# A graph network with attention on one core: where GpSimd adds the output bias and forms block sums

## The chip, the core and the metric

The kernel runs on one core of one Trainium2 chip. The time is the device time of one execution in microseconds (us); lower is better. TensorE (PE) multiplies into PSUM banks, ScalarE (ACT) and VectorE (DVE) read them out, GpSimd (POOL) works on SBUF alone here, and SyncE (SP) issues nearly all DMAs. Each engine works through its own queue in order and waits on semaphores.

## The reference

Everything is float32. `N` is 1024 nodes, `D` 512, there are `L` = 4 layers, 8 heads and 16 graphs of 64 nodes with 256 condition rows each.

```python
h = relu(layernorm(x)); x_in = h
h = batchnorm(h) * bn_w + bn_b
h = gcn(h, src, dst, gcn_in_w, gcn_in_b)
for i in range(4):
    a = attn(ln(h, ln2_w[i], ln2_b[i]), cond, Wq[i], Wk[i], Wv[i], Wo[i])
    h = h + a
    u = ln(h, ln3_w[i], ln3_b[i]) @ geglu_w[i] + geglu_b[i]      # 512 -> 4096
    val, gate = split(u, 2)
    f = val * gelu(gate)                                         # exact gelu
    h = h + f @ ffo_w[i] + ffo_b[i]                              # 2048 -> 512
h = gcn(h, src, dst, gcn_out_w, gcn_out_b)
return x + h + x_in
```

The bias `ffo_b[i]` is a term of a sum: it may be added to `h` anywhere behind the layer's second normalisation (`ln3`) and ahead of the next layer's first (`ln2`).

## The kernel before, in words

**Products.** Nearly every product is written as seven block products in place of eight (a fast scheme over 2 x 2 blocks). Each operand needs three or four extra sums or differences of its blocks ahead of the product, and VectorE adds the results up as they leave PSUM. The operand sums are what GpSimd mostly does:

- `weight_sums` (L220 to L223, tiles `wks`, `wvs`, `wqs`) for the attention's weights,
- `wo_sums` (L838, into the tile `wos`) for the output projection,
- `sum_first` (`sums_of_b`, L213 to L216, tiles `ln2T`, `ln2S`) for the normalised rows; blocks 0 and 1 on GpSimd, 2 and 3 on VectorE,
- `pair_sums` (L848 to L851) and parts of `attn_out_pair` for the attention's output,
- `ln3_sums` (tiles `ln3T`, `ln3S`) behind the second normalisation,
- `geglu_weights` (L220 to L223, tiles `ges`), `inner_left` (tiles `gi`), `inner_right` (L987, into `wos` once the attention no longer needs it) and `out_weights` (tiles `wffs`) for the feed-forward part.

**A layer.** `h` lies in SBUF as eight row blocks of 128 (`h[0]` to `h[7]`, views of the tile `hall`).

1. *Start of a layer.* For every layer but the first: `weight_sums` for the queries, `sum_first` of blocks 0 and 1 on GpSimd, then `kv(l, 0, ...)`: the keys of the first group, on VectorE behind their last copy `ready_first(l, left_to_turn[2:])` (mean, variance, reciprocal root in some ten steps on 128x2 numbers at L134 to L143, and the scaled rows at L172), and the values. Then `turn_first` transposes the four blocks left over, VectorE makes the sums of blocks 2 and 3 (L213 to L216), and `queries` follows. `wo_sums` is issued behind the last of the GpSimd sums (`summed`).
2. *Attention.* A loop over `g` = 0 to 7, a group being two graphs. Behind the keys of group `g + 1` the function `between` adds the attention's output of two earlier blocks to `h` and normalises the blocks in `ready` (`ln3_norm`): block `g - 2`, and blocks 4 and 5 when `g` is 6. Blocks 6 and 7 are normalised behind the loop.
3. *Feed-forward part*, in four quarters `r` = 0 to 3 of the 2048 inner columns. In each, `geglu` makes the gated product and `ffn_out` multiplies it by the quarter's `ffo_w` and adds into `h` in two halves `s` (blocks 0, 1, 4, 5 and blocks 2, 3, 6, 7; L1116). In the quarter `r` = 0 the gated product is made by four quads (`Quad.rest`, L938 to L957; the last operation, L957, is returned by the lambda). Behind each quad VectorE makes a block sum of the result (L1085, or L1087 to L1089). In the quarters `r` >= 1 it is made by two pairs (`Pair.run`), in which two of the seven block products (`INNER`, 5 and 6) are again split into seven (`Pair.seven`); these need `inner_left` sums of the weights, new in each quarter, and `inner_right` sums of the normalised rows, which are made once, behind the first quarter, and kept in `wos`. L1063, L964 and L968 are VectorE's additions in a pair.

Behind the first quarter's `geglu.last` (L1089) GpSimd makes `geglu_weights` for `r` = 1, then `inner_blocks` (left and right), `out_weights` for `r` = 1, and in `r` = 1 the eight bias adds at L1405. They are written ahead of the second quarter's pairs:

```python
            if r == 1:
                for nb in range(NB):
                    nc.gpsimd.tensor_tensor(h[nb], h[nb], ffb, OP.add)
```

**Order.** The order of each queue comes from the order of the program text, priorities, and two helpers. `tc.issue_after(ins)` puts what is inside behind an instruction in the queues. `waiting_for(ins, engine)` makes every instruction of that engine inside it wait for `ins` by a semaphore. SBUF tiles come from pools of fixed size, so a load waits until the tile that lay there before is done with; the biases `ffb` and `bias_out` share the pool `rows` with two places, and the next layer's `ffb` is loaded when the one before it has been used.

Of the kernel before, what the change touches and what calls it, by code (L numbers as in the profile page):

```python
# [14 lines left out]
OP = mybir.AluOpType  # L15
# [8 lines left out]
def gnn_kernel(  # L24
# [26 lines left out]
    nc = tc.nc  # L51
# [3 lines left out]
    BS, M, DC = cond.shape  # L55
# [162 lines left out]
    def sums_of_a(t, a11, a12, a21, a22, s1, s2, s4):  # L218

        t.tensor_tensor(s1, a21, a22, OP.add)  # L220
        t.tensor_tensor(a21, a11, a21, OP.subtract)
        t.tensor_tensor(s2, s1, a11, OP.subtract)
        t.tensor_tensor(s4, a12, s2, OP.subtract)  # L223

    def halves_of(t):
        return t.rearrange("p (a b) -> p a b", a=2)
# [474 lines left out]
    def weight_sums(w, name):  # L701

        s = slots_of(2, name)
        blk = blocks_of_w(w)
        s1, s2, s4 = (halves_of(s[i // 2][:, i % 2, :]) for i in range(3))
        sums_of_a(nc.gpsimd, *blk, s1, s2, s4)
        return [blk[0], blk[1], s4, blk[3], s1, s2, blk[2]]

    def seven(name, product, c11, c12, c21, c22, s1=None, beside=lambda ins: None,
# [273 lines left out]
    def inner_right(t, y, t1, t2, t3, t4):  # L983

        b11, b12, b21, b22 = (y[:, k, n * M:(n + 1) * M] for k in range(2) for n in range(2))
        for to, of, less in ((t1, b12, b11), (t3, b22, b12), (t2, b22, t1), (t4, b21, t2)):
            t.tensor_tensor(to, of, less, OP.subtract)  # L987
        return [b11, b21, b22, t4, t1, t2, t3]

    INNER = (5, 6)  # L990

    def inner_blocks(l, r, left, right, rights):

        rooms = [t512(f"gi_{l}_{r}_{i}") for i in range(3)]
        rooms = [x[:, i * M:(i + 1) * M] for x in rooms for i in range(2)]
        kept = [wos[:, n, i * M:(i + 1) * M] for n in range(4) for i in range(2)]
        lefts = {}
        for n, i in enumerate(INNER):
            if not r:
                rights[i] = inner_right(nc.gpsimd, right[i], *kept[4 * n:4 * n + 4])  # L1000
            lefts[i] = inner_left(nc.gpsimd, left[i], *rooms[3 * n:3 * n + 3])
        return lefts

    class Pair:

# [73 lines left out]
    def geglu(quads, fT, s, begun, beside=lambda c: None):  # L1079
        def sums(c):  # L1080
            k = c % 2
            a11, a12, a21, a22 = (fT[i][j][:, k, :] for i in range(2) for j in range(2))
            s1, s2, s4 = (x[:, k, :] for x in s)
            if c < 2:
                nc.vector.tensor_tensor(a21, a11, a21, OP.subtract)  # L1085
            else:
                nc.vector.tensor_tensor(s2, a22, a21, OP.subtract)  # L1087
                nc.vector.tensor_tensor(s1, s2, a11, OP.add)
                sums.last = nc.vector.tensor_tensor(s4, a12, s2, OP.subtract)  # L1089

        for c, q in enumerate(quads):
            if begun:
                q.rest()()
                beside(c)
                sums(c)
            else:
                q.run(sums, beside)
        geglu.last = sums.last
        return order7([*fT[0], *fT[1]], *s)
# [165 lines left out]
    for l in range(L):  # L1265

        wk, wv, wq, wo, ffb = projections
        if l:
            wq = weight_sums(wq, f"wqs_{l}")
            lnS = slots_of(3, f"ln2S_{l}")  # L1270
            sum_first(nc.gpsimd, 0)
            summed = sum_first(nc.gpsimd, 1)
            kv_next = kv(l, 0, wk, wv, lambda _: ready_first(l, left_to_turn[2:]))
            turn_first(l, left_to_turn)
            next_cond(l, 1)
            sum_first(nc.vector, 2)
            sum_first(nc.vector, 3)
        else:
            lnS = slots_of(3, f"ln2S_{l}")
            roots = []  # L1280

            def root_beside(ins):
                with tc.issue_after(ins.ins):
                    roots.append(deviations(mv_first[1], "ln2_0_4"))

            kT, last_key = keys(0, 0, wk, begun["k0"], root_beside)
            with tc.issue_after(last_key.ins):
                scale_first(1, *roots)
            turn_first(0, [0, 1, 2, 3])
            with waiting_for(scale_first.last, mybir.EngineType.Pool):  # L1290
                wq = weight_sums(wq, "wqs_0")
            kv_next = kT, values(0, 0, wv, begun["v0"])
            turn_first(0, [4, 5, 6, 7])
            sum_first(nc.gpsimd, 0)
            summed = sum_first(nc.gpsimd, 1)
            kT_1, last_key = keys(0, 1, wk, begun["k1"])
            with tc.issue_after(last_key.ins):
                sum_first(nc.vector, 2)
                sum_first(nc.vector, 3)
# [19 lines left out]
        def ln3_sums(t, nb):  # L1319
# [2 lines left out]
            of = [ln3T[i][k][:, :, c0:c0 + P] for k in range(2) for i in range(2)]  # L1322
            sums_of_b(t, *of, *(x[:, :, c0:c0 + P] for x in ln3S), nc.gpsimd)

        oTs = []
        for g in range(NG - 1):
            kT, v = kv_next
            if g == NG - 2:
                raw = load_geglu(l, 0)
            if l == 0:  # L1330
                fetch_cond(g + 2)
            probs = scores(l, g, qT, kT)
            ready = [g - 2, g - 1] if g == NG - 2 else [g - 2] if g > 1 else []

            def between(last_key):
                nonlocal left
                if len(oTs) == 2:
                    blocks = pair_sums(l, g - 2, oTs)
                    oTs.clear()
                    if g == NG - 2:  # L1340
                        with waiting_for(scores.last, mybir.EngineType.Pool):
                            left = geglu_weights(l, 0, *raw)
                    attn_out_pair(l, g - 2, *blocks, wo7)
                ln3_norm(*ready, behind=last_key)

            if g or l:
                kv_next = kv(l, g + 1, wk, wv, between, late=lambda: [ln3_turn(nb) for nb in ready])
            else:
                kv_next = kT_1, values(0, 1, wv)
            save_conds()  # L1350
            next_cond(l, g + 2)
            for nb in ready:
                if nb >= 4:
                    ln3_sums(nc.gpsimd, nb)
            oTs.append(mix(l, g, probs, v))
# [42 lines left out]
        for r in range(R):  # L1398
            if r:
                wff = out_weights(nc.gpsimd, l, r, raw_out)  # L1400
            else:
                raw_out = load_out(l, 0)
            if r == 1:
                for nb in range(NB):
                    nc.gpsimd.tensor_tensor(h[nb], h[nb], ffb, OP.add)  # L1405
            if r + 1 < R:
                raw = load_geglu(l, r + 1)
            beside = lambda c: None
            if r:
                fT, fS, quads = pairs_of(l, r, left, right, (lefts, rights))  # L1410
                nb = 2 * (l * (R - 1) + r - 1)
                if nb < NB:
                    if nb == 0:
                        bias_out = load_row(gcn_out_b, 0, "bias_out")
                        nc.gpsimd.tensor_tensor(x_shift, x_mean.rearrange(
                            "p a (b c) -> p (a b) c", c=2)[:, :, 0], x_root, OP.mult)
                        nc.gpsimd.tensor_scalar(x_shift, x_shift, -1.0, None, OP.mult)
                    fetch_x(nb)
                    fetch_x(nb + 1)
                    beside = lambda p: base_of(nb + p)  # L1420
            else:
                wff = []
                beside = lambda c: wff.extend(
                    out_weights(nc.vector, l, 0, raw_out) if c == 2 else [])
            fT = geglu(quads, fT, fS, not r, beside)
            if r + 1 < R:
                raw_out = load_out(l, r + 1)
                with waiting_for(geglu.last, mybir.EngineType.Pool):
                    left = geglu_weights(l, r + 1, *raw)
                    lefts = inner_blocks(l, r, left, right, rights)  # L1430
                for s in range(2):
                    ffn_out(l, r, s, fT, wff, kept)
            else:
                lnT = [slots_of(2, f"ln2T_{l + 1}_{i}") for i in range(2)]
                if last:
                    w_out, base = load_last()
                else:
                    projections = load_projections(l + 1)
                ffn_out(l, r, 0, fT, wff, kept)
                ready_first(l + 1, [0, 1, 4, 5])  # L1440
                ffn_out(l, r, 1, fT, wff, kept)
                turn_first(l + 1, [0, 1, 4, 5])
                left_to_turn = [2, 3, 6, 7]
                ready_first(l + 1, left_to_turn[:2])
# [58 lines left out]
```

## Time and profile before

| | us |
|---|---|
| median of three runs | 2542.27 |
| lowest and highest of them | 2540.95, 2543.8 |
| the profiled execution, its own time | 2546.36 |
| its span in the trace | 2544.6 |
| busy in the span: TensorE | 2498.3 |
| VectorE | 1519.7 |
| GpSimd | 614.7 |
| ScalarE | 533.4 |

The mean granted TensorE clock over the span is 0.996. In the rows of the profile, "L1405" is a line of the kernel, "x7" a number of instructions that a row merges, and `hall<-hall,ffb` the tile written and the tiles read. In a timeline the first two numbers are the start from the span's begin and the time taken, and what stands in brackets is the idle time ahead of the row on its engine and who ended it. In the waits the numbers are the sum, how often, and the longest. In the groups the first two numbers behind the bar are the busy time and the mean of one in ns, and behind the second bar stands the idle time ahead of the group.

### The profile page before, as it was taken

Reading aid. Unit: us, or ns where it says so; the run is one execution under the profiler, and the core shown is the slowest. Engines: PE = TensorE matmul, PEld = TensorE weight load, DVE = VectorE, ACT = ScalarE, POOL = GpSimd, SP = SyncE. Lnnn points to the kernel's source line nnn. Section 1 sums busy time; section 2 is a strip of 40 time slices with the busy share of each in tenths; the row PEclk is TensorE's granted clock in tenths of the full one; section 3 lists DMA queues with packets and bytes.
Section 4 is the critical chain, followed back from the end, with each engine's and each line's share of the span. In section 5 each row is a group of like instructions: output and inputs, shape, how many; then the busy total and the mean of one; then the engine's idle time right before and its main releaser. Section 6 shows DMA issues by size and latency. Waiting matters only on the chain. (4 is left out here: it accounts for less than half of the span.)

```text
span 2544.6 us, 33047 instructions
## 1 busy us (share of the span) xinstructions
PE 2498.3 (98%) x12752; PEld 1824.1 (72%) x12752; DVE 1519.7 (60%) x3298; ACT 533.4 (21%) x1318; POOL 614.7 (24%) x581
## 2 busy tenths in 40 slices
PE   7999999999999999999999999999999999999999
PEld 5778886666668887666677888566677888566665
DVE  9655565656764555666584555655584555665561
ACT  7322222111112222111112222210112222211111
POOL 1322222544310003352420003053420002153300
PEclk9999999999999999999999999999999999999999
DMA  6302231111211122110202211110121122111210
GB/s 178 130 29 92 92 128 51 42 67 33 103 52 65 59 63 67 42 67 17 96 29 75 71 63 56 44 42 26 50 75 58 47 70 67 42 42 50 83 34 34
DMA packets 69380, 161.06 MB, mean 63 GB/s; under 512 B 5768, under 2 KB 6096, under 8 KB 69216
## 3 DMA queue, kind: packets, MB, share of 16 engines
q1 hardware_dynamic: 67120, 153.44, 18.5%
q0 software_dynamic: 1376, 4.30, 0.5%
q8 instruction: 105, 1.72, 0.3%
q10 hardware_dynamic: 720, 1.11, 0.1%
q14 instruction: 59, 0.48, 0.1%
HBM read 135.76 MB, written 23.07 MB: 62 GB/s over the span
## 5 line engine op out<-in xcount | busy, mean ns | idle before, releaser
L302 PE MATMUL ga<-ln3T,wval 128*128 128x512 f32 x512 | 246.5, 595 | 0.0
L302 PEld LDWEIGHTS ga<-ln3T,wval 128*128 128x128 f32 x512 | 96.4, 191 | 90.4 <-issue 86.5
L933 ACT ACTIVATE g<-g,gcols 128x512 f32<-128x512 f32 x128 | 87.2, 716 | 341.4 <-DVE g L964 113.8
L777 ACT ACTIVATE pr<-sc,nmax 128x256 f32<-128x256 f32 x256 | 118.0, 473 | 176.7 <-DVE nmax L772 176.7
L848 POOL TENSOR_TENSOR os<-oT 128x256 f32<-128x256 f32 x12 | 8.7, 728 | 586.3 <-DVE oT L823 586.3
L220 POOL TENSOR_TENSOR ges<-wgate,wgate 128x1024 f32<-128x1024 f32 x16 | 37.7, 2356 | 412.6 <-DVE fs L1089 312.4
L302 PE MATMUL pd_k<-ct,wks 128*128 128x256 f32 x512 | 125.1, 389 | 8.8 <-DVE y_ln L136 8.8
L302 PE MATMUL gd<-ln3T,ges 128*128 128x512 f32 x256 | 123.5, 605 | 9.7 <-DVE g L964 9.6
L302 PE MATMUL gd<-ln3S,ges 128*128 128x512 f32 x256 | 128.1, 592 | 0.0
L302 PE MATMUL pa_v<-wv,ct 128*128 128x256 f32 x512 | 124.1, 382 | 0.0
L302 PE MATMUL fa<-wff,fT 128*128 128x256 f32 x512 | 121.6, 379 | 0.0
L302 PE MATMUL pc_v<-wv,ct 128*128 128x256 f32 x512 | 121.0, 379 | 0.0
L302 PE MATMUL pc_k<-ct,wk 128*128 128x256 f32 x512 | 121.0, 379 | 0.0
L302 PE MATMUL pd_v<-wvs,ct 128*128 128x256 f32 x512 | 120.9, 379 | 0.0
L302 PE MATMUL gc<-ln3S,wgate 128*128 128x512 f32 x256 | 120.3, 592 | 0.0
L302 PEld LDWEIGHTS pd_k<-ct,wks 128*128 128x128 f32 x512 | 99.4, 195 | 23.9 <-issue 9.9
L302 PE MATMUL pa_k<-ct,wk 128*128 128x256 f32 x480 | 116.2, 385 | 0.0
L302 PEld LDWEIGHTS fa<-wff,fT 128*128 128x128 f32 x512 | 97.3, 190 | 21.8 <-issue 8.9
L302 PEld LDWEIGHTS pa_v<-wv,ct 128*128 128x128 f32 x512 | 98.1, 192 | 14.0 <-issue 0.4
L302 PEld LDWEIGHTS pc_k<-ct,wk 128*128 128x128 f32 x512 | 97.3, 190 | 13.2
L302 PEld LDWEIGHTS pd_v<-wvs,ct 128*128 128x128 f32 x512 | 97.3, 190 | 13.2
L302 PEld LDWEIGHTS pc_v<-wv,ct 128*128 128x128 f32 x512 | 95.7, 190 | 12.2
(354 smaller groups left out, 5079.4 us busy)
## 6 DMA issues: line engine op xcount, KB each, us to landing
ct<-cond_dram SPq DMA_DIRECT2D x72, 512.0 KB, 4.4
wval<-in_L_gnn_geglu_w_dram SPq DMA_DIRECT2D x32, 512.0 KB, 3.8
wgate<-in_L_gnn_geglu_w_dram SPq DMA_DIRECT2D x32, 512.0 KB, 4.7
wff<-in_L_gnn_ffo_w_dram SPq DMA_DIRECT2D x32, 512.0 KB, 4.1
cond_dram<-ct SPq DMA_DIRECT2D x24, 512.0 KB, 3.2
cond<-in_L_gnn_cond_dram SPq DMA_DIRECT2D x32, 256.0 KB, 4.5
ct<-cond_dram SPq DMA_DIRECT2D x24, 256.0 KB, 5.4
wk<-in_L_gnn_Wk_dram SPq DMA_DIRECT2D x8, 512.0 KB, 4.6
```

The costliest lines, as they stand in the source:

```text
L220: t.tensor_tensor(s1, a21, a22, OP.add)
L302: nc.tensor.matmul(at, left[:, k, l0:l1], right[:, k, r0:r1], start=start and n == 0 and k == 0, stop=n == len(cols_of) - 1 and k == 1, sk ...
L777: nc.scalar.activation(pr3[:, a, :], ps3[:, a, :], AF.Exp, bias=nmax[:, a:a + 1], accum_out=tot[:, a:a + 1])
L848: t.tensor_tensor(s1, a21, a22, OP.add)
L933: nc.scalar.activation(pre, pre, AF.Gelu, bias=gcols[:, cg:cg + 1])
```

## The change

1. **Output bias.** The eight adds of `ffb` to `h` in the quarter `r` = 1 are gone. `add_bias` adds it to a block on GpSimd right behind that block's second normalisation in the attention (blocks 0 to 5), and for blocks 6 and 7 behind the first quarter's gated product, together with the sums for `r` = 1. In the built queue of GpSimd these two stand second and fifth there, between the four `ges` sums.
2. **Right sums.** `inner_blocks` is divided. The left sums stay where they were. The right sums are made during the first quarter: those of product 5 wait for quad 0's last operation, those of product 6 for quad 1's.
3. **First sums of a layer** (layers 1 to 3). `sum_first` of blocks 0 and 1 and the queries' `weight_sums` are written behind `kv(l, 0, ...)` and wait for `scaled.last`, the last scaled rows of the layer's first normalisation. `wo_sums` now comes behind the last of the queries' weight sums.

TensorE, ScalarE and VectorE keep their instructions and, but for one exchange of two neighbouring products in the first quarter's output and of the two additions that belong to them, their order. In SyncE's queue the load of the next layer's `ffb` moves, in layers 0 and 1, from behind the weights for `r` = 2 to ahead of the two loads `x_again` that stand before those weights.

```diff
@@ sums_of_a
-        t.tensor_tensor(s4, a12, s2, OP.subtract)
+        return t.tensor_tensor(s4, a12, s2, OP.subtract)
@@ weight_sums
-        sums_of_a(nc.gpsimd, *blk, s1, s2, s4)
+        weight_sums.last = sums_of_a(nc.gpsimd, *blk, s1, s2, s4)
@@
-    def inner_blocks(l, r, left, right, rights):
-
+    def inner_lefts(l, r, left):
         rooms = [t512(f"gi_{l}_{r}_{i}") for i in range(3)]
         rooms = [x[:, i * M:(i + 1) * M] for x in rooms for i in range(2)]
-        kept = [wos[:, n, i * M:(i + 1) * M] for n in range(4) for i in range(2)]
-        lefts = {}
-        for n, i in enumerate(INNER):
-            if not r:
-                rights[i] = inner_right(nc.gpsimd, right[i], *kept[4 * n:4 * n + 4])
-            lefts[i] = inner_left(nc.gpsimd, left[i], *rooms[3 * n:3 * n + 3])
-        return lefts
+        return {i: inner_left(nc.gpsimd, left[i], *rooms[3 * n:3 * n + 3])
+                for n, i in enumerate(INNER)}
+
+    def inner_right_of(n, right):
+        rooms = [wos[:, 2 * n + k, i * M:(i + 1) * M] for k in range(2) for i in range(2)]
+        return inner_right(nc.gpsimd, right[INNER[n]], *rooms)
@@ geglu
-                q.rest()()
+                q.last = q.rest()()
@@ start of a layer
         if l:
-            wq = weight_sums(wq, f"wqs_{l}")
             lnS = slots_of(3, f"ln2S_{l}")
-            sum_first(nc.gpsimd, 0)
-            summed = sum_first(nc.gpsimd, 1)
             kv_next = kv(l, 0, wk, wv, lambda _: ready_first(l, left_to_turn[2:]))
+            with waiting_for(scaled.last, mybir.EngineType.Pool):
+                sum_first(nc.gpsimd, 0)
+                sum_first(nc.gpsimd, 1)
+                wq = weight_sums(wq, f"wqs_{l}")
+                summed = weight_sums.last
             turn_first(l, left_to_turn)
@@ attention
+        def add_bias(nb):
+            nc.gpsimd.tensor_tensor(h[nb], h[nb], ffb, OP.add)
+
@@ between
                 ln3_norm(*ready, behind=last_key)
+                for nb in ready:
+                    add_bias(nb)
@@ quarters
-            if r == 1:
-                for nb in range(NB):
-                    nc.gpsimd.tensor_tensor(h[nb], h[nb], ffb, OP.add)
@@
                 wff = []
-                beside = lambda c: wff.extend(
-                    out_weights(nc.vector, l, 0, raw_out) if c == 2 else [])
+
+                def beside(c):
+                    if c == 2:
+                        wff.extend(out_weights(nc.vector, l, 0, raw_out))
+                    elif c < 2:
+                        with waiting_for(quads[c].last, mybir.EngineType.Pool):
+                            rights[INNER[c]] = inner_right_of(c, right)
+
             fT = geglu(quads, fT, fS, not r, beside)
             if r + 1 < R:
                 raw_out = load_out(l, r + 1)
                 with waiting_for(geglu.last, mybir.EngineType.Pool):
                     left = geglu_weights(l, r + 1, *raw)
-                    lefts = inner_blocks(l, r, left, right, rights)
+                    lefts = inner_lefts(l, r + 1, left)
+                    if not r:
+                        for nb in range(NB - 2, NB):
+                            add_bias(nb)
```

## The prediction

> **What bounds the kernel now.** I read the page first, then the waits of TensorE, then the granted clock around each wait, then the timeline in front of each.
>
> ```profile
> PE 2498.3 (98%) x12752; PEld 1824.1 (72%) x12752; DVE 1519.7 (60%) x3298; ACT 533.4 (21%) x1318; POOL 614.7 (24%) x581
> ```
>
> TensorE is busy for 98% and the queues of its work stay as they are, so a change elsewhere can only move the 2% in which it waits, and what follows a wait. Who it waits for:
>
> ```profile
> PE gd L302 <- DVE g L964: 9.6, 4, 2.4
> PE pd_k L302 <- DVE y_ln L136: 8.8, 3, 3.0
> PE tr_ln L184 <- DVE xn_ln L172: 5.4, 4, 1.7
> ```
>
> The first is one wait per layer, the second one per layer but the first. Both are VectorE being late. A wait also costs after its end, which the windows show (the column behind the busy times is PEclk, the granted clock):
>
> ```profile
> 508.00:513.00 5.00, 4.73 (x7) 2.01 (x8) 3.13 (x6) 2.65 (x4) 1.89 (x2) 0.66 0.03 11
> 709.00:714.00 5.00, 4.49 (x25) 4.07 (x26) 4.79 (x14) 2.94 (x7) 2.85 (x5) 1.00 0.08 30
> 1100.00:1105.00 5.00, 4.42 (x11) 2.03 (x12) 4.03 (x5) 2.65 (x4) 1.57 (x2) 1.00 0.08 22
> 1905.00:1910.00 5.00, 4.34 (x13) 3.63 (x14) 4.33 (x15) 0.00 (x0) 0.00 (x0) 0.66 0.01 3
> ```
>
> A mean of 0.66 over 5 us is 3.4 us at half clock: 5 x 0.34 = 1.7 us of TensorE's work lost. It came behind two of the four L964 waits (508 is the first; behind 1100 there is none) and all three L136 waits (1905 is the last), five in all: 8.5 us. Behind the shorter tr_ln wait (709) the clock stayed at 1.00. The Trainium skill (TensorE: Matmul & The Clock Gate, "Part 1: The HAM clock gate") says that the gate halves the clock after about one idle window of 3.4 us; by that no wait of 2.4 to 3.0 us would lower it and the 8.5 us would be left out of the sum. The trace differs: 2.4 us were enough twice, so the rows decide.
>
> **Why VectorE is late in the second quarter (r = 1).**
>
> ```profile
> 497.20 8.61 POOL L1405 TENSOR_TENSOR hall<-hall,ffb 128x512 f32<-128x512 f32 x7
> ...
> 502.51 3.85 DVE L1063 TENSOR_TENSOR gw<-gw,gw 128x512 f32<-128x512 f32 x1
> ...
> 508.27 2.83 PE L302 MATMUL gd<-ln3T,ges 128*128 128x512 f32 x4 [2.39 <-DVE g L964]
> ...
> 530.08 0.69 DVE L1063 TENSOR_TENSOR gw<-gw,gw 128x512 f32<-128x512 f32 x1
> ```
>
> L1063 adds two SBUF tiles. It takes 0.69 us when GpSimd is idle (530.08) and 3.85 us while seven bias adds run: it ends 0.55 us after their end at 505.81. TensorE's wait of 2.39 us is shorter than the 3.16 us that L1063 loses, so without the adds L964 is 0.8 us early.
>
> **Why it is late at a layer's start.**
>
> ```profile
> 715.41 0.60 DVE L139 SCALAR_TENSOR_TENSOR a_ln<-y_ln,v_ln 128x2 f32<-128x2 f32 x1
> ...
> 716.85 1.19 DVE L139 SCALAR_TENSOR_TENSOR a_ln<-y_ln,v_ln 128x2 f32<-128x2 f32 x1
> ...
> 718.56 0.70 DVE L141 TENSOR_TENSOR b_ln<-a_ln,y_ln 128x2 f32<-128x2 f32 x1
> ...
> 719.21 2.61 POOL L838 TENSOR_TENSOR wos<-wo,wos 128x512 f32<-128x512 f32 x2
> ...
> 719.29 1.20 DVE L143 SCALAR_TENSOR_TENSOR y_ln<-b_ln,y_ln 128x2 f32<-128x2 f32 x1
> ...
> 720.72 1.11 DVE L141 TENSOR_TENSOR b_ln<-a_ln,y_ln 128x2 f32<-128x2 f32 x1
> ...
> 722.98 0.69 DVE L728 TENSOR_TENSOR kT<-pd_k,u_k 128x512 f32<-128x512 f32 x1
> ...
> 723.77 0.16 DVE L139 SCALAR_TENSOR_TENSOR a_ln<-y_ln,v_ln 128x2 f32<-128x2 f32 x1
> 723.81 3.28 PE L302 MATMUL pd_k<-ct,wks 128*128 128x256 f32 x8 [2.86 <-DVE y_ln L136]
> ...
> 725.61 1.00 DVE L172 TENSOR_SCALAR xn_ln<-hall,mv_ln,y_ln 128x512 f32<-128x512 f32 x2
> ...
> 743.18 0.41 DVE L213 TENSOR_TENSOR ln2S<-ln2T,ln2T 128x256 f32<-128x256 f32 x1
> ```
>
> The steps of the reciprocal root work on 128x2 numbers in SBUF: 0.16 us each once GpSimd is done (723.77), up to 1.2 us while its sums run. The five shown lose 0.60 + 1.19 + 0.70 + 1.20 + 1.11 - 5 x 0.16 = 4.0 us. L728, behind them in VectorE's queue, reads the bank that pd_k overwrites; it ends at 723.67 and pd_k starts 0.14 us later. The wait named "y_ln L136" is thus L728. 4.0 us earlier it ends at 719.7, and TensorE would have wanted it at 723.81 - 2.86 = 720.95: the wait goes with 1.1 us to spare.
>
> **The change part by part.** The prices of GpSimd's work:
>
> ```profile
> L1405 POOL TENSOR_TENSOR hall<-hall,ffb 128x512 f32<-128x512 f32 x32 | 39.5, 1268 | 0.0
> L987 POOL TENSOR_TENSOR wos<-ln3S 128x256 f32<-128x256 f32 x8 | 5.8, 728 | 0.0
> L220 POOL TENSOR_TENSOR wqs<-wq,wq 128x512 f32<-128x512 f32 x4 | 5.1, 1270 | 80.7 <-PE gd L302 72.8 <-DVE xn_ln L172 8.0
> L848 POOL TENSOR_TENSOR os<-oT 128x256 f32<-128x256 f32 x12 | 8.7, 728 | 586.3 <-DVE oT L823 586.3
> ```
>
> *A. No bias adds in r = 1.* The eight adds (10 us of GpSimd) go; so do the eight right sums from the run ahead of them (5.8 us), and two adds (2.5 us) come into it. GpSimd is then done about 497.2 - 5.8 + 2.5 = 494, before 502.5. Gain 9.6 us of waits and 2 x 1.7 = 3.4 of clock: 13.0.
>
> *B. Sums held behind the last normalised rows.* GpSimd stands still until L172 is done, which without the stretched steps is 726.6 - 4.0 = 722.6. Queued behind that wait: eight sums of 128x256 (8 x 0.73 = 5.8), four of wq (4 x 1.27 = 5.1), four of wo (two took 2.61 above: 5.2), 16.1 us, done about 738.7. VectorE does only PSUM work in that time. Who waits: the queries, which need VectorE's own ln2S sums too, from 743.18 on, or 738.6 in the new time (2.9 us of wait and 1.7 of clock earlier). GpSimd is done at that moment, so at worst its last sum holds L213: 1.3 us in each of three layers, 4 us. I take nothing, since the two ends meet. Gain 8.8 + 3 x 1.7 = 13.9.
>
> *C. Right sums beside the first quarter.* Four sums (2.9 us) start when quad 0, and again quad 1, has its last product, while VectorE goes on with the quad's SBUF work. This is the new cost.
>
> ```profile
> 441.91 0.75 DVE L957 SCALAR_TENSOR_TENSOR fT<-ga,gcols,g 128x512 f32<-128x512 f32 x1
> ...
> 443.17 0.68 DVE L1085 TENSOR_TENSOR fT<-fT,fT 128x512 f32<-128x512 f32 x1
> ...
> 443.88 0.69 DVE L943 TENSOR_TENSOR gu<-gc,gu 128x512 f32<-128x512 f32 x1
> ...
> 445.39 1.88 PE L302 MATMUL gc<-ln3S,wgate 128*128 128x512 f32 x4
> ...
> 450.30 0.69 DVE L956 TENSOR_TENSOR fT<-gv,g 128x512 f32<-128x512 f32 x1
> ...
> 452.46 0.69 DVE L943 TENSOR_TENSOR gu<-gc,gu 128x512 f32<-128x512 f32 x1 [0.28 <-PE gc L302]
> ...
> 453.98 1.88 PE L302 MATMUL gc<-ln3S,wgate 128*128 128x512 f32 x4
> ```
>
> Behind quad 0 the sums run from about 442.8 to 445.6 and meet L1085; L943 behind it must end before TensorE's gc at 445.39, and has 0.82 us to spare. Behind quad 1 they meet L956 and L1085, with 0.83 us to spare. Low end: each meeting costs one GpSimd sum (0.73), as L143 and L141 above got in at the end of each L838: nothing behind quad 0, 2 x 0.73 - 0.83 = 0.6 behind quad 1, 2.5 us in four layers. High end: VectorE waits for all four, as L1063 did for a run of seven: L1085 ends at 446.3, L943 at 447.0, 1.7 us late; behind quad 1 about 1.3; 3.0 x 4 = 12 us. I take 2.5, because L838 is the same formula (its last sum needs the one before), while the seven adds were independent of each other. The Trainium skill (SBUF — State Buffer, "SBUF: two separate sides") says that the two engines share a port pair as a lock that is held for one whole instruction. By that rule the low end holds. The L1063 row speaks against it, having missed the ends of several adds, so the high end stays a rival.
>
> *D. The moved bias adds.* Six of eight a layer go behind the attention's normalised rows, where GpSimd waits 586 us in all for oT (L848): 7.6 us a layer of idle time, beside PSUM work of VectorE. Nothing. Two go second and fifth in GpSimd's queue behind the first quarter:
>
> ```profile
> 470.88 2.35 POOL L220 TENSOR_TENSOR ges<-wgate,wgate 128x1024 f32<-128x1024 f32 x1 [38.88 <-DVE fs L1089]
> ...
> 481.80 0.69 DVE L1116 TENSOR_TENSOR hall<-fc,hall 128x512 f32<-128x512 f32 x1 [2.76 <-PE fc L302]
> ...
> 486.78 1.89 PE L302 MATMUL fc<-wffs,fT 128*128 128x256 f32 x8
> ```
>
> Three sums of 2.35 and two adds of 1.27 end at 470.88 + 9.6 = 480.5. VectorE's first add into blocks 6 and 7 is at 481.80 (1.3 us to spare), and TensorE needs its bank only at 486.78. Nothing.
>
> *E. SyncE.* In layers 0 and 1 the next layer's ffb load now stands ahead of the x loads and the weights for r = 2, and waits for that last bias add (480.5):
>
> ```profile
> 510.16 0.80 ACT L1392 ACTIVATE again<-x_again,x_shift,x_root 128x512 f32<-128x512 f32 x1
> ```
>
> The x rows are then still issued 29 us before ScalarE reads them at 510.16, and the weights are for a quarter later. Nothing.
>
> **Sum.** 13.0 + 13.9 - 2.5 = 24.4 us. The profiled execution's 2546.36 us would become 2522.0; the three runs' median is 4.1 us lower, 2542.27, and gives 2517.9: 2518.
>
> **Rivals.** *1. The right sums take back half:* part C at its high end, 2542.3 - 26.9 + 12 = 2527.4. For it: the 3.85 us of L1063. Against: the last of four needs the one before. *2. Only one of the two waits goes:* VectorE's chain at a layer's start stays late for a reason of its own (its room is 1.1 us), so B's 13.9 are missing: 2531.8; or A's 13.0: 2530.9. Against both: the same operations run at 0.16 and 0.69 us with GpSimd quiet. *3. Slower: the two late bias adds hold up the second half of the first quarter's output.* They stand behind the weight sums, and those have also waited for room in SBUF:
>
> ```profile
> POOL ges L220 <- DVE fs L1089: 312.4, 8, 50.6
> POOL ges L220 <- PE fa L302: 74.0, 2, 37.8
> ```
>
> If the sums at r = 0 had to wait for the output's products instead of for L1089, they would start about 487 rather than 470.88, the add into blocks 6 and 7 could start about 497, and TensorE would stand from 486.78: 10 us and 1.7 of clock a layer, 47 us in four, 2565. It decides from the third layer on, when 35 us exceed the gain. Against: the 470.88 row was released by L1089. *4. The schedule makes nothing of it:* 2542. Against: in the built order the adds are gone from r = 1 and the wq sums stand behind the first ln2S sums.
>
> **How the numbers follow.** Forecast 0.62 (2518, by itself 2513 to 2522); rival 1 0.17; rival 2 0.11; rival 3 0.06; rival 4 0.04. The forecast and rivals 1 and 2 are faster by over 0.2% (5.1 us, about what a measurement can tell): 0.90; same 0.04; slower 0.06. The range runs from the whole 26.9 with 2 us of spread below (2513) to just short of both forms of rival 2 (2530), which leaves out about 0.2.
>
> **What would show it.** Right: no L964 wait of TensorE in r = 1, L1063 at 0.69 everywhere there, root steps at 0.16 behind each layer's first keys, no half clock at these places. Wrong: a wait of gc for L943 in the first quarter with L1085 or L956 above 1.4 us (rival 1), pd_k still waiting (rival 2), or fc waiting for hall at L1116 (rival 3).

## The result: 25.8 us less, and the profile after

| | before | changed |
|---|---|---|
| median, us (four runs each) | 2543.03 | 2517.22 |
| lowest and highest, us | 2540.95, 2545.92 | 2517.09, 2517.43 |
| the profiled execution, us | 2546.36 | 2517.15 |
| its span, us | 2544.6 | 2515.4 |

The ratio is 0.9898, with a 95% interval of 0.9881 to 0.9915: 1% faster. When the two kernels were measured again later, beside the last experiment, it was 0.9892 (0.9875 to 0.9908). The prediction was 2518. The line numbers of the changed kernel differ a little: L1083 is what was L1085, L1085 to L1087 were L1087 to L1089, L1061 was L1063, L1114 was L1116, and L1326 is the line of `add_bias`.

From the page of the changed kernel, busy time by engine:

```profile
PE 2488.1 (99%) x12752; PEld 1821.3 (72%) x12752; DVE 1487.5 (59%) x3298; ACT 534.0 (21%) x1318; POOL 619.7 (25%) x581
```

VectorE has the same 3298 instructions and is busy for 32 us less: 12 us of it in L1063, 13 in the root steps (L139 to L143) and 7 in the sums at L1087 to L1089, all of which had taken longer while GpSimd worked. TensorE is busy for 10 us less with the same 12752 matmuls: mostly the five stretches at half clock, 8.5 us. Its waits in the changed kernel (sum, times, longest):

```profile
PE tr_ln L184 <- DVE xn_ln L172: 5.1, 3, 1.7
...
PE gd L302 <- DVE g L964: 0.6, 1, 0.6
```

The four L964 waits of 2.4 us and the three pd_k waits of 2.9 us are gone. What is left of L964 is one wait of 0.6 us, in another quarter (`r` = 3 of the first layer), where sums for the next layer's weights meet L1061. The later profile of the same kernel doesn't have it.

The second quarter's start in the first layer: GpSimd's run ends at 490.97, and L1061 comes 9.4 us later and takes 0.69 us, as it does every time in this quarter.

```profile
489.70 1.27 POOL L216 TENSOR_TENSOR wffs<-wff,wffs 128x512 f32<-128x512 f32 x1
...
500.33 0.69 DVE L1061 TENSOR_TENSOR gw<-gw,gw 128x512 f32<-128x512 f32 x1
```

The start of the second layer, in the changed kernel's timeline:

```profile
711.03 0.16 DVE L141 TENSOR_TENSOR b_ln<-a_ln,y_ln 128x2 f32<-128x2 f32 x1
...
711.23 0.16 DVE L143 SCALAR_TENSOR_TENSOR y_ln<-b_ln,y_ln 128x2 f32<-128x2 f32 x1
...
712.34 0.68 DVE L728 TENSOR_TENSOR kT<-pd_k,u_k 128x512 f32<-128x512 f32 x1
...
714.75 1.89 PE L302 MATMUL pd_k<-ct,wks 128*128 128x256 f32 x8
...
716.12 1.41 POOL L213 TENSOR_TENSOR ln2S<-ln2T,ln2T 128x256 f32<-128x256 f32 x2 [41.66 <-DVE xn_ln L172]
...
729.10 2.62 POOL L838 TENSOR_TENSOR wos<-wo,wos 128x512 f32<-128x512 f32 x2
...
730.31 7.03 PE L302 MATMUL qa<-ln2T,wq 128*128 128x512 f32 x16
...
732.36 0.41 DVE L213 TENSOR_TENSOR ln2S<-ln2T,ln2T 128x256 f32<-128x256 f32 x1
...
737.18 1.88 PE L302 MATMUL qb<-ln2S,wqs 128*128 128x512 f32 x4
```

The root steps take 0.16 us. L728 ends at 713.02, and pd_k starts at 714.75, without a wait and with 1.7 us of room. GpSimd starts its first sums when L172 is done and ends the last at 731.72, 0.6 us ahead of VectorE's first L213.

The first quarter, behind quad 0 and behind quad 1, where the right sums (L987) are now made:

```profile
440.63 1.86 POOL L987 TENSOR_TENSOR wos<-ln3S 128x256 f32<-128x256 f32 x2 [10.79 <-DVE fT L957]
...
440.99 0.91 DVE L1083 TENSOR_TENSOR fT<-fT,fT 128x512 f32<-128x512 f32 x1
...
441.82 0.68 DVE L943 TENSOR_TENSOR gu<-gc,gu 128x512 f32<-128x512 f32 x1
...
443.22 1.88 PE L302 MATMUL gc<-ln3S,wgate 128*128 128x512 f32 x4
...
447.51 1.89 POOL L987 TENSOR_TENSOR wos<-ln3T 128x256 f32<-128x256 f32 x2 [3.52 <-DVE fT L957]
...
448.12 0.69 DVE L956 TENSOR_TENSOR fT<-gv,g 128x512 f32<-128x512 f32 x1
...
449.33 0.68 DVE L1083 TENSOR_TENSOR fT<-fT,fT 128x512 f32<-128x512 f32 x1
...
449.36 2.04 POOL L987 TENSOR_TENSOR wos<-ln3T,wos 128x256 f32<-128x256 f32 x2
...
450.29 0.69 DVE L943 TENSOR_TENSOR gu<-gc,gu 128x512 f32<-128x512 f32 x1 [0.28 <-PE gc L302]
...
451.80 1.88 PE L302 MATMUL gc<-ln3S,wgate 128*128 128x512 f32 x4
```

VectorE loses 0.22 us once (L1083, 0.91 in place of 0.69). Here it is GpSimd that is stretched: two sums of 0.73 take 1.86, 1.89 and 2.04 us. TensorE has no gc wait in any layer.

### The profile page after: what moved, and what is told of

It reads as the page before. It is cut to its first block, busy times and chain, and to the rows that moved or that the text cites. A ratio compares the mean times of both kernels' runs of the same rounds, so it can differ in the third digit from the quotient of the medians.

```text
span 2515.4 us, 33075 instructions
## 1 busy us (share of the span) xinstructions
PE 2488.1 (99%) x12752; PEld 1821.3 (72%) x12752; DVE 1487.5 (59%) x3298; ACT 534.0 (21%) x1318; POOL 619.7 (25%) x581
## 5 line engine op out<-in xcount | busy, mean ns | idle before, releaser
L302 PEld LDWEIGHTS pa_k<-ct,wk 128*128 128x128 f32 x480 | 88.7, 190 | 21.3 <-issue 10.4
```

Of the source, the lines that this page charges most:

```text
L302: nc.tensor.matmul(at, left[:, k, l0:l1], right[:, k, r0:r1], start=start and n == 0 and k == 0, stop=n == len(cols_of) - 1 and k == 1, sk ...
```

## The experiments

All were compared with the kernel before on the same chip, where its median was between 2543.7 and 2544.1 us. Unless it says otherwise, an edit is made to the changed kernel.

**Each half of the change by itself.** First with only the held sums kept:

```diff
-                for nb in ready:
-                    add_bias(nb)
...
+            if r == 1:
+                for nb in range(NB):
+                    nc.gpsimd.tensor_tensor(h[nb], h[nb], ffb, OP.add)
...
-                    elif c < 2:
-                        with waiting_for(quads[c].last, mybir.EngineType.Pool):
-                            rights[INNER[c]] = inner_right_of(c, right)
...
-                    lefts = inner_lefts(l, r + 1, left)
-                    if not r:
-                        for nb in range(NB - 2, NB):
-                            add_bias(nb)
+                    lefts = inner_blocks(l, r, left, right, rights)
```

> The changed kernel with the bias adds and the right sums put back where they were; only the held first sums of a layer are kept. Theory (each of the two waits is GpSimd work beside VectorE's SBUF work, and the two are independent): the four L964 waits of 2.4 us and two half clocks return, pd_k's wait stays gone: 13.0 us over the changed kernel, 2530. Rival (the two places share one cause, so that undoing one loses more or less than its part): pd_k waits again (2544), or no L964 wait returns (2517).

Then with the first sums of a layer back where they were:

```diff
+            wq = weight_sums(wq, f"wqs_{l}")
             lnS = slots_of(3, f"ln2S_{l}")
+            sum_first(nc.gpsimd, 0)
+            summed = sum_first(nc.gpsimd, 1)
             kv_next = kv(l, 0, wk, wv, lambda _: ready_first(l, left_to_turn[2:]))
-            with waiting_for(scaled.last, mybir.EngineType.Pool):
-                sum_first(nc.gpsimd, 0)
-                sum_first(nc.gpsimd, 1)
-                wq = weight_sums(wq, f"wqs_{l}")
-                summed = weight_sums.last
```

> The changed kernel with a layer's first GpSimd sums where they were (wq sums ahead of the layer, blocks 0 and 1 without the wait). Theory: root steps of VectorE up to 1.2 us again, pd_k waits 3 x 2.9 us and the half clock follows three times: 13.9 us over the changed kernel, 2531. Rival (VectorE's chain was late for a reason of its own that the other edits removed): 2517, root steps at 0.16.

Measured: 2531.55 (ratio 0.9953, 0.9936 to 0.9969) and 2531.7 (0.9953, 0.9937 to 0.997) beside 2543.68. TensorE's waits of the first:

```profile
PE gd L302 <- DVE g L964: 9.6, 4, 2.4
PE tr_ln L184 <- DVE xn_ln L172: 5.4, 4, 1.7
```

and of the second:

```profile
PE pd_k L302 <- DVE y_ln L136: 8.9, 3, 3.0
PE tr_ln L184 <- DVE xn_ln L172: 5.1, 3, 1.7
```

Each half takes away its own wait and leaves the other whole, and the gains of 12.1 and 12.0 us add up to about that of the change. Rival 2 falls.

**Which of the two moves ahead of `r` = 1 does it.** With the bias adds back in `r` = 1 and the right sums still beside the first quarter (the first, second and last part of the first diff above, with `inner_lefts` kept):

> The changed kernel with only the eight bias adds put back into the second quarter; the right sums stay beside the first quarter. Theory (it is only a matter of when GpSimd's run ends): without the right sums the run ends about 505.8 - 5.5 = 500.3 in the time of before, 2.2 us ahead of L1063, so nothing returns: 2517. Rival (the adds into h themselves hold VectorE or TensorE up, wherever they end): the L964 waits return, 2530.

With the right sums back behind the first quarter, and the two bias adds put ahead of that run of sums:

```diff
                 with waiting_for(geglu.last, mybir.EngineType.Pool):
-                    left = geglu_weights(l, r + 1, *raw)
-                    lefts = inner_lefts(l, r + 1, left)
                     if not r:
                         for nb in range(NB - 2, NB):
                             add_bias(nb)
+                    left = geglu_weights(l, r + 1, *raw)
+                    if not r:
+                        rights.update({INNER[n]: inner_right_of(n, right) for n in range(2)})
+                    lefts = inner_lefts(l, r + 1, left)
```

> The changed kernel with only the right sums put back into the run behind the first quarter; the adds to blocks 6 and 7 are put ahead of that run. Theory: GpSimd is done about 498.7 in the time of before, 3.8 us ahead of L1063, and the place beside the first quarter costs and saves nothing: 2517. Rival (the place beside the first quarter costs the 2.5 us of the prediction, which something else has given back): 2514.7.

Measured: 2515.96 (0.9892, 0.9875 to 0.9908) and 2515.45 (0.9889, 0.9873 to 0.9906) beside 2543.68. No pd_k wait and no L964 wait of `r` = 1 in either. The two moves are not both needed: either one lets GpSimd's run end before L1061 begins. In the first layer it ends at 498.4 and L1061 starts at 500.2 with the first move undone; with the second undone the two are 496.6 and 500.5. What the right sums cost beside the first quarter can't be read from the second time alone, since 2515.45 lies between its two forecasts (2517 and 2514.7). But the kernel that keeps them there is as fast within the spread of its runs (2515.04 to 2516.66, against 2515.12 to 2516.18), and neither trace has a gc wait, so they cost about half a us at most.

**The adds late, as in rival 3.** The right sums go back, and the order of the text then puts the two bias adds behind the sums for `r` = 1:

```diff
-                    elif c < 2:
-                        with waiting_for(quads[c].last, mybir.EngineType.Pool):
-                            rights[INNER[c]] = inner_right_of(c, right)
...
+                    if not r:
+                        rights.update({INNER[n]: inner_right_of(n, right) for n in range(2)})
```

> The changed kernel with the right sums back behind the first quarter; the scheduler then puts the two bias adds of blocks 6 and 7 behind all the weight and block sums of r = 1 instead of between the first of them. In the time of the kernel before, GpSimd reaches the second of these adds at about 470.9 + 22.7 = 493.6, while TensorE wants the bank that VectorE's add into blocks 6 and 7 frees at 486.78. Theory (rival 3 of the prediction: an add late enough holds up the second half of the first quarter's output): TensorE waits at fc for about 7 us and loses 1.7 us of clock in each of four layers, 35 us: about 2552, slower than the kernel before. Rival (the queue in between has enough slack): no wait of fc, about 2517.

Measured: 2557.0 (1.005, 1.0034 to 1.0067), slower than the kernel before. Of its timeline, its waits, and its windows (the number behind GpSimd's busy time is the granted clock):

```profile
490.68 1.26 POOL L1326 TENSOR_TENSOR hall<-hall,ffb 128x512 f32<-128x512 f32 x1
...
491.97 0.69 DVE L1114 TENSOR_TENSOR hall<-fc,hall 128x512 f32<-128x512 f32 x1 [14.51 <-POOL hall L1326]
...
492.72 3.78 PE L302 MATMUL fc<-wffs,fT 128*128 128x256 f32 x8 [7.34 <-DVE hall L1114]
```

```profile
PE fc L302 <- DVE hall L1114: 29.5, 4, 7.4
```

```profile
488.00:490.00 2.00, 0.00 (x0) 0.00 (x0) 0.00 (x0) 0.00 (x0) 2.00 (x3) 0.50 0.00 0
490.00:492.00 2.00, 0.00 (x0) 0.00 (x0) 0.03 (x1) 0.00 (x0) 2.00 (x4) 0.50 0.00 0
...
496.00:498.00 2.00, 2.00 (x6) 1.55 (x5) 0.69 (x1) 0.00 (x0) 1.08 (x1) 0.50 1.05 401
498.00:500.00 2.00, 2.00 (x8) 1.39 (x7) 0.69 (x1) 0.00 (x0) 0.00 (x0) 0.97 1.03 396
```

The second add ends at 491.94, VectorE stands for 14.5 us in front of its add into those rows, and with it TensorE for 7.3. The clock falls inside the wait and stays at half until 498.1, 5.4 us after the products go on: 2.7 us of work, not 1.7. In the third layer it is 3.3 us; all four together lose 9.8 us of work. 29.5 + 9.8 = 39.3 us is close to the 40 us over the changed kernel that were measured. So the effect that rival 3 foresaw is real. The cause that it named, weight sums that wait for the output's products, is not what was built here, and in the changed kernel GpSimd's `ges` sums never wait for `fa`. In the changed kernel the adds stand second and fifth in that run, and the time hangs on that place.

**Do the weight sums of the queries have to be held?** Only the sums of the rows stay behind the wait; `weight_sums` goes back ahead of `kv`.

```diff
+            wq = weight_sums(wq, f"wqs_{l}")
...
-                sum_first(nc.gpsimd, 1)
-                wq = weight_sums(wq, f"wqs_{l}")
-                summed = weight_sums.last
+                summed = sum_first(nc.gpsimd, 1)
```

> The changed kernel with the queries' weight sums back at the end of the layer before; only the first sums of the rows stay held behind the last normalised rows. Theory (the root steps are met by the first row sums and the wo sums, and those stay behind the wait): no pd_k wait, about 2517; the sums of the queries' weights may stretch VectorE's L1087 to L1089 as before, with no wait of TensorE for it. Rival (the weight sums' place was what counted): the three pd_k waits of 2.9 us and three half clocks come back, about 2531.

Measured: 2516.05 (0.989, 0.9873 to 0.9906) beside 2543.93. No pd_k wait. In the groups of VectorE its L1085 has a mean of 776 ns, as against 687 in the changed kernel:

```profile
L1085 DVE TENSOR_TENSOR fs<-fT,fT 128x512 f32<-128x512 f32 x32 | 24.8, 776 | 0.5
```

The weight sums again stretch VectorE at the end of the layer before, and TensorE waits for none of it. Holding them is no part of the gain.

**What in GpSimd's run holds VectorE up.** Four kernels put work at the place that the bias adds have left, the first three in layers 2 and 3 only. The first adds a chain of twelve adds into a scratch tile, the second thirty memsets of it:

```diff
+            if r == 1 and l > 1:
+                scratch = t512(f"scratch_{l}")
+                for i in range(12):
+                    nc.gpsimd.tensor_tensor(scratch, scratch if i else ffb, ffb, OP.add)
```

> The changed kernel with 12 more GpSimd adds in r = 1 of layers 2 and 3, each into the same scratch tile that the next one reads (a chain); nothing of the result is touched. They take the place of the bias adds in time but not in what they touch. Theory (two engines that read SBUF meet, whatever the tiles; a chain lets VectorE in at the end of the running add): VectorE's L1063, which meets them, takes at most about 0.7 + 1.3 = 2.0 us and TensorE's L964 wait is 0.5 us or less. Rival A (VectorE waits for the whole run, chain or not): L1063 takes over 3 us, and L964 waits of 2 us or more come back in those two layers (about 7 us with the clock: 2524). Rival B (it was the tile h, not the port): L1063 at 0.69 and no wait.

```diff
+                for i in range(30):
+                    nc.gpsimd.memset(scratch, 0.0)
```

> The changed kernel with 30 GpSimd memsets of a scratch tile in r = 1 of layers 2 and 3: GpSimd works as long there but only writes SBUF. Theory (what meets are the reads of SBUF): L1063 stays at 0.69 us, no L964 wait, about 2517. Rival (any GpSimd work in SBUF holds up a VectorE add of two SBUF tiles): L1063 above 1 us, and TensorE waits for L964 of up to 2.4 us in those two layers (up to 2524).

Measured: 2517.56 and 2515.76 (one run each). The timeline with the chain:

```profile
1666.18 1.36 DVE L1061 TENSOR_TENSOR gw<-gw,gw 128x512 f32<-128x512 f32 x1
...
1667.98 1.24 DVE L1061 TENSOR_TENSOR gw<-gw,gw 128x512 f32<-128x512 f32 x1
...
1669.99 1.98 PE L302 MATMUL gd<-ln3T,ges 128*128 128x512 f32 x4 [0.44 <-DVE g L964]
```

GpSimd's adds around the first L1061, singly:

```profile
1665.72 1.27 POOL L1411 TENSOR_TENSOR scratch<-scratch,ffb 128x512 f32<-128x512 f32 x1
...
1667.07 1.59 POOL L1411 TENSOR_TENSOR scratch<-scratch,ffb 128x512 f32<-128x512 f32 x1
```

And the timeline with the memsets:

```profile
1656.67 15.66 POOL L1411 MEMSET scratch<- 128x512 f32 x27
...
1665.79 0.69 DVE L1061 TENSOR_TENSOR gw<-gw,gw 128x512 f32<-128x512 f32 x1
...
1667.15 0.69 DVE L1061 TENSOR_TENSOR gw<-gw,gw 128x512 f32<-128x512 f32 x1
```

L1061 met the memsets with at most 0.15 us of the running one left, or in a pause of 0.06 us between two, so its 0.69 us alone says little. But the memsets that ran beside it took their usual 0.52 us:

```profile
1665.99 0.52 POOL L1411 MEMSET scratch<- 128x512 f32 x1
```

An add beside L1061 takes 1.59 in place of 1.27. So memsets, which only write, neither hold VectorE up nor are held up by it. With adds, L1061 waits although no tile is shared, but only for the add that is running: that one ends at 1666.99, the next begins 0.08 us later, L1061 is in and ends at 1667.54, and now the next add is the long one (1.59).

The third kernel takes away the pause: two scratch tiles by turns, so that no add needs the one just before it.

```diff
-                scratch = t512(f"scratch_{l}")
+                scratch = [t512(f"scratch_{l}_{i}") for i in range(2)]
                 for i in range(12):
-                    nc.gpsimd.tensor_tensor(scratch, scratch if i else ffb, ffb, OP.add)
+                    s = scratch[i % 2]
+                    nc.gpsimd.tensor_tensor(s, s if i > 1 else ffb, ffb, OP.add)
```

> As the kernel with twelve chained adds in r = 1 of layers 2 and 3, but the twelve go by turns into two scratch tiles, so that an add never needs the one just before it. In the chained kernel GpSimd stood 0.08 us between two adds and VectorE's L1063 (L1061 in this kernel) got in there: 1.36 us, and TensorE waited 0.44 us. Theory now (VectorE gets in only where GpSimd pauses between two instructions, and independent adds leave no pause): L1061 waits for the end of the whole run, 5 to 6 us, and TensorE waits about 4.5 us for L964 in each of the two layers with 1.7 us of clock behind it: about 12 us over the changed kernel, 2529. Rival (VectorE gets in at every instruction's end, and what held it up in the kernel before was that the adds wrote h): L1061 at 1.4 us, TensorE's wait 0.4 us, 2517.

Measured: 2529.69 (one run). The timeline:

```profile
1659.60 12.28 POOL L1412 TENSOR_TENSOR scratch<-scratch,ffb 128x512 f32<-128x512 f32 x10
...
1667.14 5.30 DVE L1061 TENSOR_TENSOR gw<-gw,gw 128x512 f32<-128x512 f32 x1
...
1672.88 0.69 DVE L1061 TENSOR_TENSOR gw<-gw,gw 128x512 f32<-128x512 f32 x1
...
1673.60 0.69 DVE L964 TENSOR_TENSOR g<-gd,gw 128x512 f32<-128x512 f32 x1
...
1674.35 3.78 PE L302 MATMUL gd<-ln3T,ges 128*128 128x512 f32 x4 [3.84 <-DVE g L964]
```

Ten adds of 1.26 us in 12.28: they overlap by a few hundredths, and L1061 stands until the run ends at 1671.88. It missed three ends of adds on the way. TensorE waits 3.84 us in the first of the two layers and 3.85 in the second, where 4.5 were expected.

The last of the four goes back to the kernel before, with its eight adds where they were, and makes each wait for the one before it:

```diff
-                for nb in range(NB):
-                    nc.gpsimd.tensor_tensor(h[nb], h[nb], ffb, OP.add)
+                added = nc.gpsimd.tensor_tensor(h[0], h[0], ffb, OP.add)
+                for nb in range(1, NB):
+                    with waiting_for(added, mybir.EngineType.Pool):
+                        added = nc.gpsimd.tensor_tensor(h[nb], h[nb], ffb, OP.add)
```

> The kernel before with one thing changed: each of its bias adds in r = 1 waits by a semaphore for the add before it (the same eight adds, at the same place, and their run no shorter). Theory (what holds VectorE up is that the adds follow each other without a pause; a wait between them leaves one of about 0.08 us, and VectorE gets in there): L1063 at most 1.4 us, TensorE's L964 wait 0.5 us or less in each of four layers and no half clock behind it; the pd_k waits stay. 9.6 us of waits less 4 x 0.44, and 3.4 us of clock: about 11 us under the kernel before, 2532. Rival (the pause is not what counts): L1063 at 3.8 us and 2543.

Measured: 2530.17 (0.9948, 0.9931 to 0.9965) beside 2543.66. Its timeline (L1063 is the kernel before's line):

```profile
495.14 10.02 POOL L1407 TENSOR_TENSOR hall<-hall,ffb 128x512 f32<-128x512 f32 x7
...
500.22 0.79 DVE L1063 TENSOR_TENSOR gw<-gw,gw 128x512 f32<-128x512 f32 x1
...
501.58 1.10 DVE L1063 TENSOR_TENSOR gw<-gw,gw 128x512 f32<-128x512 f32 x1
```

GpSimd's run is longer and its adds are the same, yet the L964 waits and the half clock behind them are gone. A semaphore between the adds does what moving them did.

**The wait that is left.** Blocks 4 and 5 are transposed behind the first keys instead of ahead of them:

```diff
-            kv_next = kv(l, 0, wk, wv, lambda _: ready_first(l, left_to_turn[2:]))
+            def first_rows(_):
+                turn_first(l, [4, 5])
+                ready_first(l, left_to_turn[2:])
+            kv_next = kv(l, 0, wk, wv, first_rows)
...
-                turn_first(l + 1, [0, 1, 4, 5])
+                turn_first(l + 1, [0, 1, 4, 5] if last else [0, 1])
```

> The changed kernel with blocks 4 and 5 transposed behind the first group's keys instead of at the end of the layer before, aimed at the tr_ln wait that is left (1.7 us in each of three layers). Theory: the keys start 1.7 us earlier, VectorE is not yet late for pd_k (L728 ended 1.7 us ahead of pd_k, of which 1.7 us are used up), and the time falls by 5.1 us below the changed kernel run beside it: about 2512. Rival (the wait only moves): pd_k waits for L728 by what VectorE's later copies cost, and the time stays at 2517.

> The changed kernel itself, on the same chip as the kernel with the later transposes, to compare the two: 2517.

Measured: 2510.28 (0.9868, 0.9852 to 0.9885), and the changed kernel beside it 2516.85 (0.9892, 0.9875 to 0.9908), before 2544.1. This is the fastest version here.

```profile
708.79 0.69 DVE L728 TENSOR_TENSOR kT<-pd_k,u_k 128x512 f32<-128x512 f32 x1
...
711.89 1.89 PE L302 MATMUL pd_k<-ct,wks 128*128 128x256 f32 x8
```

The tr_ln waits are gone and pd_k's room is 2.4 us, not nothing: four of VectorE's copies behind those transposes (L697, eight ahead of L728 in the changed kernel and four here) went out of L728's way too. 5.1 us of the 6.6 are the tr_ln waits of the three layers; what the rest is was not looked for.

## Why the prediction was right, point by point

**A, no bias adds in `r` = 1: right, for the reason given.** Waits and half clocks were put at 13.0 us; by itself, with the right sums moved, this half gave 12.0. What the prediction could not say is which move is needed. Either one is enough, since with either GpSimd's run ends before L1061 starts; the kernel before with a pause between its adds shows that the run need not even end.

**B, held sums: right.** 13.9 us were forecast. By itself this half gave 12.1, in a run in which the clock fell behind three of the four remaining L964 waits and not behind two, which is 1.7 us of the difference. The room of 1.1 us for L728 was 1.7. GpSimd's last sum ended 0.6 us ahead of L213 where the two ends were expected to meet.

**C, the right sums: the term that was mis-sized.** 2.5 us were taken, as the low end, four times 0.6 behind quad 1, and it was about nothing. The step that failed is that each of two meetings there costs VectorE a whole GpSimd sum, 2 x 0.73. (It also left out the 0.28 us for which L943 stood idle in its own row, waiting for a product, which is room too.) L956 and L1083 both came as a sum was ending (448.24 and 449.40), lost nothing, and it was GpSimd's next sum that was held off; nobody was waiting for that. Behind quad 0, where nothing was forecast for TensorE, L1083 came halfway through the first sum and lost 0.22. The sum without C, 26.9 us, lies between the 25.8 and 27.3 that the two comparisons gave.

**Where luck helped.** 2518 is nearer to 2517.22 than its terms deserve. The forecast gain of 24.4 us is 1.4 to 2.9 short, mostly by C, and the base of 2542.27 that it was taken from was 0.8 to 1.8 us below the medians measured later. The five half clocks in the sum are those of one execution; in others the clock fell behind more or fewer waits (see the last section).

**D and E: right.** The second bias add ends at 478.1 and VectorE's add into its rows starts at 479.7, 1.6 us of room where 1.3 were forecast, and TensorE has no wait for `hall` or for a load in the layers.

**The rivals.** 1 (the right sums take back half) fell with the gc rows above. Its ground was sound, though: a run of adds can hold VectorE up to its end, as the twelve adds into two scratch tiles showed. 2 fell with the two halves. 3 did not happen here, and its effect is real: with the adds later in the same run the kernel is at 2557.0. Its price was put at 11.7 us a layer and is 10.0. Against it the prediction named the row at 470.88, released by L1089; what kept the second half free was also that the adds stood second and fifth in that run, as part D had them, not twentieth and twenty-second. 4 falls with the measured time.

**The clock.** The Trainium skill (TensorE: Matmul & The Clock Gate, "Part 1: The HAM clock gate") gives an idle window of about 3.4 us behind which the clock is halved. With that as the least wait that counts the sum would have been 15.9 us. The traces differ: the windows show half clock behind waits of 2.4 us. The two halves, 12.1 and 12.0, are also more than their waits of 8.8 and 9.6, though the intervals, some 4 us either way, would not settle that by themselves.

## What to carry to other kernels

When an instruction takes several times its usual time, look at what the neighbour engine does in that stretch before looking at its inputs. What helped here was to let the neighbour's run end earlier, start later, or pause between its instructions. Before moving an add to a "free" place on another engine, find the next reader or writer of that tile: two such adds too late in the queue cost more here than the whole change brought. Price a meeting on both engines, since either can be the one that waits, and only one of them is on the path.

## What had not been expected of the hardware

- **A pause of 0.08 us decides.** VectorE's adds of two SBUF tiles got in at the first pause between two GpSimd instructions: 1.36 us (0.69 without GpSimd), against 5.30 in a run without pauses. Without a pause it was never let in between adds of the `ffb` kind, but mostly was between block sums, as at L1083 above and at the root steps of the kernel before. What tells these apart (the kind of operation, the operands, their addresses) is open; no run separated them.
- **Memsets do not meet VectorE's adds.** With thirty memsets in place of twelve adds L1061 took 0.69 us and the memsets beside it 0.52, as without it. That it is the reading that counts fits this; no other instruction that only writes was tried.
- **A wait's price in clock depends on where it falls.** Behind waits of 2.4 us the clock fell in two of four cases in the kernel before and in three of four with only the held sums. Behind 2.9 to 3.0 us it fell in eight of nine: in the kernel before and with its adds in a chain each time, with the first sums back in two of three. Behind 1.7 us it never fell. In each trace the stretches at half clock begin whole multiples of 3.413 us apart; in the kernel before 509.26, 724.30 and 1314.81 are 63 and 173 of them apart. On that grid the first wait of 2.4 us lies in one step and the second in two (of the view's columns, the step, its length, the busy time of TensorE and, third from the end, the granted clock):

```profile
505.85:509.26 3.41, 1.02 (x4) 0.51 (x4) 3.27 (x6) 0.95 (x2) 0.00 (x0) 1.00 0.22 77
1096.35:1099.77 3.42, 1.83 (x5) 0.52 (x3) 3.32 (x3) 0.00 (x0) 1.77 (x2) 1.00 0.12 32
1099.77:1103.18 3.41, 2.60 (x6) 1.25 (x7) 2.49 (x5) 2.56 (x4) 0.00 (x0) 1.00 0.17 44
```

  TensorE stands for 2.39 us of the first step, and the next step, from 509.26, is at half clock. It stands for 1.59 and 0.81 us of the other two, and no half clock follows. In all fourteen traces a step at full clock in which TensorE stood for 2.1 us or more was followed by half clock (19 of 19), one with 1.75 us or less never; of seven with 1.9 us six were. So which waits counted was chance. This was read from the traces; no run moved a wait to test it. Behind 7.3 us the clock fell inside the wait, and the half clock lasted 3.3 to 5.6 us into the work.
